# Transposing expert activations on VectorE in squares of 32, with ScalarE putting the squares together

## The chip, the cores and the metric

The kernel runs on one core of one Trainium2 chip. The metric is the time on the device in microseconds (us). Each number called "time before" is the median of three runs. Beside the runs there is one profiled execution, from which all durations of single instructions come.

## The reference, cut to what matters

The model is one block with two layers on an input of 4 x 1024 tokens of 1024 features. The first layer is a two-sided scan over time that gates a dense layer. The second layer, where the change lies, is a mixture of experts:

```python
logits = flat @ router_w.T                      # 4096 tokens, E = 32 experts
topk_w, topk_ids = lax.top_k(softmax(logits), 4)
xs = take(flat, tok_idx)                        # tokens sorted by expert
g, u = split(ragged_dot(xs, w1, group_sizes), 2)    # w1: 1024 x (2 * 512) per expert
act = silu(g) * u
ys = ragged_dot(act, w2, group_sizes)           # w2: 512 x 1024 per expert
routed = sum over a token's 4 experts of ys * topk_w
out = residual + routed + shared expert
```

Everything is in float32.

## The kernel before

The kernel has three stretches. In the first, up to about 1860 us, VectorE scans and TensorE computes the dense layer and the shared expert for most tokens. In the second, up to about 4644 us, the experts run. In the third, the shared expert of the last two chunks of tokens is computed.

The change is in the second stretch. Its work is cut into units. A **pair** unit (`kind` 0) takes two blocks of 128 tokens of one expert. A **single** unit (`kind` 1) takes one block. There are 68 pairs and 12 singles in a fixed list (`whole`): a single stands behind every fifth or sixth pair, and the last unit is a single. The instructions of each engine are written out by hand in the order in which that engine runs them (`manual_schedule`), so the order of the Python calls is the order on the queue of each engine.

A unit has these steps:

- `gather` fetches the tokens' rows from memory into `hs` (POOL's indirect DMAs, L904). `turn` transposes them on VectorE in squares of 32 into `hsT` (L1003). The rows are gathered in such an order that squares are enough there.
- `left_sums` forms sums of quarters of the transposed matrix (L1018 to L1022), four operations on VectorE: `s_up` from `hsT`, `s_down` from `actT`. Pairs need them because `products` multiplies two by two quarters with seven products instead of eight. `up_sums` (L870) and `down_sums` (L890) are the sums of the weights' quarters.
- `up` multiplies with w1 into the PSUM banks gA, gB and gC (L1151 for pairs, L1039 for singles), applies Silu on ScalarE (L1069, L1076, L1047), and multiplies the two halves and the token's share on VectorE (L1078, L1079, L1049). The result is `act`, 128 tokens x 512 features for each block.
- `turn_act` transposes `act`, so that the features lie on the partitions: four TensorE transposes of 128x128 for each block into a PSUM tile `tr` (L1088), and one copy on ScalarE to `actT` (L1089).
- `down` multiplies `actT` with w2 into the banks dA, dB and dC (L1151 for pairs, L1101 for singles). `add` scatters the result with an indirect DMA that adds (L1135).

In `products` (L1151) the seven products share three banks. A bank that holds a product is read by ScalarE as `m1` (L1165) or by VectorE as `u2` and `u3` (`u`, L1168 and L1174), and a later product is added into the same bank. So the second and the fourth product go to bank B, and the fourth waits until `u2` has been read out of it; the sixth takes bank A again.

`run_units` is the loop over units. It is a pipeline of two: while TensorE does `up` of unit u, VectorE works on the sums of the unit behind (`held`, whose `down` follows) and of the next one (`nxt`). The list `beside` says which steps of these sums are issued after each product of `up`. Before the change, for a pair, that is: after the first product two steps of `held.left` (the four `s_down`) and one of `held.down_sums`, after the second one more, after the third the last two, and after the fourth to the seventh one step of `nxt.up_sums` each. After `up` come the loads of w1 for the unit two ahead (SP's queue), `held.down()` with `nxt.turn()` beside it, the gather of the unit two ahead and `held.add()` on POOL, and then `turn_act` of unit u.

## Time and profile before

| What | us |
|---|---|
| Median of three runs | 4958.87 (4955.35 to 4960.45) |
| Profiled execution, its own time | 4949.14 |
| Its span | 4947.4 |
| TensorE busy (matmul) | 4654.2, 94% of the span |
| VectorE busy | 3395.2, 69% |
| ScalarE busy | 1268.3, 26% |
| Expert stretch 1850 to 4640: TensorE / VectorE / ScalarE / POOL busy | 2774.1 / 1914.7 / 304.1 / 848.4 |
| `tr` transposes of `act` on TensorE (L1088) | 592 instructions |
| `actT` copies on ScalarE (L1089) | 148 instructions, 589 ns each |

In the profile PE is TensorE, PEld its weight loads, DVE is VectorE, ACT is ScalarE, POOL is GpSimd and SP the engine that only issues DMAs. A row of a timeline gives the start, the time, the engine, the line and the operation with the tile written and the tiles read; in brackets stands how long the engine was idle before it and what ended that. A row of the chain of work that ended last gives start, time and instruction: it is followed back from the last instruction to what released it. A row of the waits gives who waited for whom: the total, the number of times and the longest.

### The profile page before, as it was taken

What the parts mean: (1) busy time and instruction counts of PE and PEld (TensorE: products, weight loads), DVE (VectorE), ACT (ScalarE), POOL (GpSimd) and SP (SyncE); (2) the same over time, 40 slices, a digit from 0 to 9 for tenths busy, and PEclk for the clock granted to TensorE, in tenths of its full rate; (3) what the DMA queues carried; (4) which work ended last, traced back from release to release, by engine and by line L of the source; (5) the groups of instructions that cost most, each with busy time, mean ns of one, the idle gap of its engine ahead of it and who ended that gap; (6) DMA issues with size and microseconds to landing.
All of it is one profiled execution on the core that took longest, in us unless ns stands there. A gap on an engine that the chain in (4) does not pass through costs nothing.

```text
span 4947.4 us, 34599 instructions
## 1 busy us (share of the span) xinstructions
PE 4654.2 (94%) x11638; PEld 2097.7 (42%) x11638; DVE 3395.2 (69%) x3579; ACT 1268.3 (26%) x1537; POOL 1230.7 (25%) x1209
## 2 busy tenths in 40 slices
PE   0379999999999999999999999999999999999999
PEld 0124444444444444444444444444444444444444
DVE  9988988898762227676767676676767676767434
ACT  5557656666451201111111111111111111111000
POOL 0013202401321212233332323233332323333000
PEclk9989999999999999999999999999999999999999
DMA  5688679669769565777777777777777777777623
GB/s 159 176 223 213 184 218 287 170 189 278 208 180 259 149 206 181 241 229 245 230 252 225 246 229 240 238 240 230 244 228 251 234 238 233 237 240 235 192 94 111
DMA packets 533886, 1071.37 MB, mean 217 GB/s; under 512 B 37537, under 2 KB 275234, under 8 KB 532866
## 3 DMA queue, kind: packets, MB, share of 16 engines
q1 hardware_dynamic: 364050, 736.31, 43.0%
q0 software_dynamic: 81760, 223.15, 21.8%
q10 hardware_dynamic: 87888, 109.59, 6.5%
q8 instruction: 94, 1.54, 0.1%
q14 instruction: 94, 0.77, 0.0%
HBM read 833.65 MB, written 205.65 MB: 210 GB/s over the span
## 4 chain that ended last, share of the span: by engine, by line
PE 85%; DVE 6%; DMA 3%; ACT 2%; issue 2%; SPq 0%; POOL 0%; ACTq 0%; DVEq 0%; POOLq 0%
PE gA L1151 15%; PE mm L660 11%; PE gC L1151 10%; PE gB L1151 10%; PE dA L1151 8%; PE mm L688 6%; PE dC L1151 6%; PE dB L1151 5%; PE mm L443 5%; PE gB L1039 2%; PE gA L1039 2%; PE tr L1088 1%; PE tr L544 1%; DVE fg L284 1%; DMA xg<-in_xT 1%
## 5 line engine op out<-in xcount | busy, mean ns | idle before, releaser
L904 POOL DMA_INDIRECT hs<-h_d,parts x584 | 591.3, 1012 | 1392.1 <-DVE hsT L1003 1237.9
L660 PE MATMUL mm<-c,wpc 128*128 128x512 f32 x1536 | 668.6, 594 | 0.0
L443 PE MATMUL mm<-c,w0t 128*128 128x512 f32 x1024 | 446.3, 597 | 209.0 <-DMA w0t<-in_w 205.8
L1151 PE MATMUL gC<-w,s_up 128*128 128x512 f32 x1184 | 532.3, 592 | 0.0
L1151 PE MATMUL gB<-t_up,s_up 128*128 128x512 f32 x1152 | 517.9, 592 | 0.0
L1151 PE MATMUL gA<-w,hsT 128*128 128x512 f32 x1088 | 491.3, 594 | 3.1 <-DVE hsT L1003 1.6
L660 PEld LDWEIGHTS mm<-c,wpc 128*128 128x128 f32 x1536 | 290.1, 191 | 356.1 <-issue 354.2
L1135 POOL DMA_INDIRECT sum_d<-y,tokens x148 | 269.3, 1820 | 589.7 <-DMA sum_d<-y,tokens 457.2
L443 PEld LDWEIGHTS mm<-c,w0t 128*128 128x128 f32 x1024 | 195.4, 192 | 456.2 <-issue 443.8
L688 PE MATMUL mm<-sact,wpc 128*128 128x512 f32 x768 | 342.5, 601 | 8.9 <-DMA wpc<-in_sd 5.7
L1151 PEld LDWEIGHTS gC<-w,s_up 128*128 128x128 f32 x1184 | 224.8, 190 | 282.2 <-issue 282.2
L1151 PEld LDWEIGHTS gB<-t_up,s_up 128*128 128x128 f32 x1152 | 218.9, 190 | 275.5 <-issue 261.6
L870 DVE TENSOR_TENSOR t_up<-w,w 128x2048 f32<-128x2048 f32 x136 | 310.6, 2284 | 0.0
L1151 PEld LDWEIGHTS gA<-w,hsT 128*128 128x128 f32 x1088 | 202.1, 191 | 232.5 <-issue 228.8
L296 DVE TENSOR_TENSOR_SCAN fg<-decay,tail,fg 128x1024 f32<-128x1024 f32 x128 | 292.7, 2328 | 0.0
L1151 PE MATMUL dB<-t_down,s_down 128*128 128x512 f32 x544 | 257.7, 596 | 9.7 <-DVE u L1168 9.7
L1151 PE MATMUL dA<-w,actT 128*128 128x512 f32 x544 | 255.6, 592 | 0.0
L1151 PE MATMUL dC<-w,s_down 128*128 128x512 f32 x544 | 255.6, 592 | 0.0
L329 POOL DMA_DIRECT2D fg<-euk x64 | 57.8, 904 | 772.9 <-DVE euk L328 509.2
L1151 PE MATMUL gA<-t_up,hsT 128*128 128x512 f32 x544 | 244.5, 592 | 0.0
L1076 ACT ACTIVATE act<-c 128x512 f32<-128x512 f32 x68 | 42.9, 630 | 708.9 <-DVE c L1072 708.9
L688 PEld LDWEIGHTS mm<-sact,wpc 128*128 128x128 f32 x768 | 145.1, 193 | 180.8 <-issue 172.8
(296 smaller groups left out, 6208.7 us busy)
## 6 DMA issues: line engine op xcount, KB each, us to landing
w<-in_w SPq DMA_DIRECT2D x240, 2048.0 KB, 8.5
fg<-euk POOLq DMA_DIRECT2D x64, 512.0 KB, 6.8
c_d<-r ACTq DMA_DIRECT2D x64, 512.0 KB, 7.7
w0t<-in_w SPq DMA_DIRECT2D x64, 512.0 KB, 6.5
c<-c_d SPq DMA_DIRECT2D x120, 256.0 KB, 6.6
wpc<-in_sg SPq DMA_DIRECT2D x48, 512.0 KB, 4.6
wpc<-in_su SPq DMA_DIRECT2D x48, 512.0 KB, 4.6
wpc<-in_sd SPq DMA_DIRECT2D x48, 512.0 KB, 6.2
```

The lines of the kernel that those rows point to most:

```text
L284: nc.vector.tensor_tensor_scan(fg[:, m, :], dk.to_broadcast([P, T]), x, 0.0, ALU.mult, ALU.add)
L296: nc.vector.tensor_tensor_scan(fg[:, m, ::-1], decay[L][:, ct, b : b + 1].to_broadcast([P, T]), fg[:, m, ::-1], tail[:, m : m + 1], ALU.mu ...
L329: nc.gpsimd.dma_start(out=num, in_=euk, accum_op=ALU.add)
L443: nc.tensor.matmul(mm, lhsT=tiles[ot][:, it, :], rhs=c0s[it], start=(it == 0), stop=(it == NC - 1))
L544: nc.tensor.matmul(lgT_ps, lhsT=rw_sb[:, ct, :], rhs=hs[ct], start=(ct == 0), stop=(ct == NC - 1))
L660: nc.tensor.matmul(mm, lhsT=wts[f, n][:, kt, :], rhs=c1s[q, kt], start=(kt == 0), stop=(kt == NC - 1))
L688: nc.tensor.matmul(mm, lhsT=wts[ct][:, f, :], rhs=acts[q, f], start=(f == 0), stop=(f == NSI - 1))
L870: nc.vector.tensor_tensor(to, x, y, ALU.subtract)
L904: nc.gpsimd.indirect_dma_start(out=to[:, bass.ts(g, C // SQ)], out_offset=None, in_=h_d.rearrange("t (q c) -> (t q) c", q=SQ), in_offset=b ...
L1039: nc.tensor.matmul(ps, lhsT=self.hsT[:, k, 0, :], rhs=w[k // NK][:, k % NK, bass.ts(n, I)], start=(k == 0), stop=(k == NC - 1),)
L1135: nc.gpsimd.indirect_dma_start(out=sum_d, out_offset=bass.IndirectOffsetOnAxis(ap=tokens[:, i, self.n : self.n + 1], axis=0), in_=y, in_of ...
L1151: nc.tensor.matmul(ps, lhsT=x[:, k, :], rhs=w[:, k, :], start=(k == 0 and not more), stop=(k == half - 1), skip_group_check=more,)
```

## The change

The activations are no longer transposed on TensorE. `turn_act` now issues one VectorE transpose for each block, of 128x512 in squares of 32, from `act` into the PSUM tile `tr`. A square stays within its 32 partitions, so ScalarE then copies from each of the four partition quadrants to each of four others: 16 copies of 32 partitions x 4 x 32 elements for each block, into `actT`. These copies are a generator, `together`, with eight steps for a pair and four for a single, each of four copies.

`run_units` issues the copies of `held` beside the `up` of the next unit: in a pair two steps after each of the first four products, in a single all steps after the two products. The `s_down` sums of `held`, which read `actT`, move from the first product to behind the sixth and the seventh, in both cases after that place's step of `up_sums`; in a single they move behind the second product. The `down_sums` move to behind the second and the third product.

```diff
             def turn_act(self):
                 self.actT = pxt.tile([P, NI, 2, P], FP, name="actT")
-                for b, act in enumerate(self.acts):
-                    tr = ps_t.tile([P, 4, P], FP, name="tr")
-                    for f in range(NI):
-                        nc.tensor.transpose(tr[:, f, :], act[:, bass.ts(f, P)], ident)
-                    nc.scalar.copy(self.actT[:, :, b, :], tr)
+                squares = []
+                for act in self.acts:
+                    squares.append(ps_t.tile([P, 4, P], FP, name="tr"))
+                    nc.vector.transpose(squares[-1].rearrange("p k t -> p (k t)"), act)
+
+                def together():
+                    for b, tr in enumerate(squares):
+                        of = tr.rearrange("p k (q j) -> p k q j", q=SQ)
+                        for r in range(SQ):
+                            for q in range(SQ):
+                                nc.scalar.copy(
+                                    self.actT[bass.ts(r, SIDE), :, b, bass.ts(q, SIDE)], of[bass.ts(q, SIDE), :, r, :]
+                                )
+                            yield
+
+                self.together = together()
                 self.left = self.left_sums(self.actT, ND, "s_down")
                 self.s_down = next(self.left, None)
...
-                jobs = [] if held is None else 2 * [held.left] + 4 * [held.down_sums]
+                jobs = [] if held is None else 4 * [held.down_sums]
+                left = [] if held is None else 2 * [held.left]
+                together = [] if held is None else 2 * [held.together]
                 sums = [] if nxt is None else 4 * [nxt.up_sums]
-                beside = [jobs + sums[:2], sums[2:]] if u.kind else [jobs[:3], jobs[3:4], jobs[4:]] + [[s] for s in sums]
+                if u.kind:
+                    beside = [2 * together + jobs + sums[:2], 2 * together + left + sums[2:]]
+                else:
+                    rest = [[s] for s in sums] if sums else [[] for _ in range(4)]
+                    beside = [together + x for x in ([], jobs[:2], jobs[2:], rest[0])] + [
+                        rest[1],
+                        rest[2] + left[:1],
+                        rest[3] + left[1:],
+                    ]
...
+            rest_of(held.together)
             rest_of(held.left)
             rest_of(held.down_sums)
```

## The prediction

> **What bounds the kernel now.** I read the page first: engine shares, then the chain of work that ended last.

> ```profile
> PE 4654.2 (94%) x11638; PEld 2097.7 (42%) x11638; DVE 3395.2 (69%) x3579; ACT 1268.3 (26%) x1537; POOL 1230.7 (25%) x1209
> PE 85%; DVE 6%; DMA 3%; ACT 2%; issue 2%; SPq 0%; POOL 0%; ACTq 0%; DVEq 0%; POOLq 0%
> ```

> TensorE bounds the kernel. The expert loop runs from 1859 to 4644 us, and between 1850 and 4640 TensorE is busy 2774.1 of 2790 us at clock 1.00, VectorE 1914.7, ScalarE 304.1. So every TensorE microsecond taken out counts, and so does every wait put in. The removed transposes, by their line, then the chain through the end of one pair unit and the start of the next (start, length):

> ```profile
> L1088 PE MATMUL tr<-ident,act x592: 272/273/421, 1885.4 to 4635.9; 128*128 128x128 f32 x198
> ```
> ```profile
> 2723.72 1.72 PE dA L1151 x4
> 2725.44 1.74 PE dB L1151 x4
> ...
> 2732.33 0.88 PE tr L1088 x8
> 2733.21 3.43 PE gA L1151 x8
> 2736.64 3.43 PE gB L1151 x8
> ```

> Eight transposes hold the chain for 0.88 us, not 8 x 0.273: they overlap, at 0.11 us each. All the rest of a pair unit is products back to back: seven of 3.43 (up), seven of 1.72 (down). Where would a wait bite? From the table of waits and the timeline of VectorE beside those products:

> ```profile
> PEld dB L1151 <- DVE u L1168: 44.5, 55, 1.7
> ```
> ```profile
> 2716.90 0.69 DVE L1072 TENSOR_TENSOR c<-u,gA 128x512 f32<-128x512 f32 x1 [0.54 <-PE gA L1151]
> 2717.50 2.28 DVE L870 TENSOR_TENSOR t_up<-w,w 128x2048 f32<-128x2048 f32 x1
> 2720.33 0.69 DVE L1072 TENSOR_TENSOR c<-u,gC 128x512 f32<-128x512 f32 x1 [0.55 <-PE gC L1151]
> 2720.93 0.75 DVE L1078 SCALAR_TENSOR_TENSOR act<-act,shares,c 128x512 f32<-128x512 f32 x1
> 2721.60 0.75 DVE L1079 SCALAR_TENSOR_TENSOR act<-act,shares,c 128x512 f32<-128x512 f32 x1
> 2722.26 2.29 DVE L870 TENSOR_TENSOR t_up<-w,t_up 128x2048 f32<-128x2048 f32 x1
> 2724.46 0.68 DVE L1168 TENSOR_TENSOR u<-m,dB 128x512 f32<-128x512 f32 x1
> ...
> 2732.37 0.69 DVE L1123 TENSOR_TENSOR y<-u,dC 128x512 f32<-128x512 f32 x1 [1.03 <-PE dC L1151]
> 2732.97 0.68 DVE L1018 TENSOR_TENSOR s_up<-hsT 128x512 f32<-128x512 f32 x1
> 2733.69 0.69 DVE L1019 TENSOR_TENSOR s_up<-s_up,hsT 128x512 f32<-128x512 f32 x1
> ...
> 2735.51 0.41 DVE L1018 TENSOR_TENSOR s_down<-actT 128x256 f32<-128x256 f32 x1
> 2735.96 0.43 DVE L1019 TENSOR_TENSOR s_down<-s_down,actT 128x256 f32<-128x256 f32 x1
> 2736.30 0.42 DVE L1021 TENSOR_TENSOR s_down<-actT 128x256 f32<-128x256 f32 x1
> ```

> The reader is to see two tight places. First, the fourth down product (the second into bank dB) waits until `u` has been read out of dB; `u` ends at 2725.14, the product starts at 2725.28, and its weight load already waited. 55 such waits are 44 pair units at 0.58 (25.5 us, hidden: the chain shows 1.74 for 1.72) and 11 single units at 1.7. So in 44 pairs VectorE is exactly in time. Second, from c to `u` VectorE runs without a gap: whatever is put there arrives late at TensorE. The start-to-start steps are 0.60 for an operation of 512 columns, 0.34 for one of 256 (0.45 if it needs the one before), 2.20 after one of 2048.

> **The change part by part.**

> *Transposes gone from TensorE: -63.1 us.* 67 pairs x 0.87 (from 2732.17, where TensorE starts the first of the eight, to gA at 2733.04) plus 11 singles x 0.44 = 58.3 + 4.8 = 63.1. The first pair gains nothing: its next product waits for hsT anyway (1.56 us, "PE gA <- DVE hsT"). The last single is priced below.

> *left_sums moved from the start of the next unit to its sixth and seventh product: +33 us.* In the changed program VectorE's order there is c, t_up, two s_down, c, act, act, t_up, two s_down, `u`. Counted from 2716.90: t_up +0.60 (2717.50), s_down +2.20 (2719.70), +0.45 (2720.15), next c 2720.49 instead of 2720.33; then 0.60, 0.67, 0.66, 2.20 to the third s_down (2724.62), 0.34, 0.34: `u` starts 2725.30 instead of 2724.46, ends 2725.98. The product starts 0.06 after `u` (as at 2095.29 and 2095.35 in a single), so 2726.04 instead of 2725.28: 0.76, call it 0.75. 44 x 0.75 = 33. Behind `u` on VectorE wait the two hsT transposes and the second `u`; they shift with the product (2728.19 against its end at 2727.9), so this is not paid twice. The 12 pairs ahead of a single have no up_sums (TensorE keeps VectorE waiting there), the 11 behind a single have no left_sums: no price.

> *VectorE's transposes, two per pair ahead of s_up: +2 us.* They stand behind y (2732.37), where TensorE's first gA now starts at 2732.17. The nearest row is hsT (L1003): 1221 ns for 1024 columns, as a TENSOR_TENSOR of that size, so 512 columns should take 0.69, step 0.60. Then s_up 2734.17, its second 2734.89, end 2735.58, gB at 2735.64 against 2735.60: 0.04 x 44 = 2. No row shows VectorE writing PSUM. Below: 0 (gB can't start before gA ends). Above: no overlap, step 0.69, 0.22 x 44 = 10. I take 0.04, since reading PSUM costs nothing (688 against 683 ns). Singles and pairs behind them have over 0.5 us of room.

> *ScalarE's copies, 16 per block, 2368 in all.* Nearest rows: 589 ns for 128x512 (L1089), 212 for 128x16 (L223), the same 575 on 32 partitions as on 128; by the line through them a 32x4x32 copy takes 0.30 us. Two in a row:

> ```profile
> 2732.81 1.07 ACT L1089 COPY actT<-tr 128x512 f32<-128x512 f32 x2 [6.74 <-PE tr L1088]
> ```

> Two of 0.59 in 1.07: they overlap by 0.11, so the step of small ones is 0.19 to 0.20. [...]

> [...]

> *Singles: +16 us.* Here all 32 copies and left_sums sit between the second up product and `u`:

> ```profile
> 2089.42 0.75 DVE L1049 SCALAR_TENSOR_TENSOR act<-act,shares,gB 128x512 f32<-128x512 f32 x1 [2.14 <-PE gB L1039]
> ...
> 2094.61 0.68 DVE L1168 TENSOR_TENSOR u<-m,dB 128x512 f32<-128x512 f32 x1
> ```

> The unit begins at 2075.41. ScalarE's Silu starts 7.07 in, copies from 7.6 to 7.6 + 32 x 0.20 = 14.0. VectorE is free at 14.68, so left_sums don't wait, and the copy m behind the copies is due only at 15.7. left_sums put 1.47 (0.45 + 3 x 0.34) ahead of the two t_up and `u`, on which dB already waits. 11 x 1.47 = 16. At a step of 0.29 the copies end at 16.9 and add 2.25 each, 25 more: 0.22 is the break point. [...]

> *The last single: +3.6 us.* Nothing runs on TensorE beside its 16 copies: y at 4635.74, transpose +0.60 to 4637.03, copies to 4640.4, dA there instead of 4636.85.

> *Nothing:* down_sums moved behind the first `u` (4 x 1.25 from 7.7 to 12.7, the second `u` is due at 13.9; were that 1.2 us of room gone, `u` and the c behind it would be late by the rest); the two PSUM tiles, which the copies free 16 us into a unit at the latest; the other queues: SP's w loads and POOL's gathers and adds keep their order and their waits on the same products, with hs gathered a unit ahead.

> Sum: -63.1 + 33 + 2 + 16 + 3.6 = -8.5 us. The profiled execution took 4949.1 (span 4947.4), 9.7 under the median 4958.87; I put the difference on the median: 4950.

> **The rivals.**
> 1. *The copies don't overlap (slower).* Place: singles, left_sums waiting for actT. Price: 352 x (step - 0.22) + 16 x (step - 0.20); at 0.29 +26, so 4976. It cancels the gain from 0.24 us a copy, and is visibly slower from 0.27. [...] Against: the overlap of the pair of copies.
> 2. *VectorE has more room than counted (faster).* If `u` were not late in the pairs, 33 us come back: 4917; with the singles too, 4901. For it: VectorE is 69% busy. Against: the 0.58 us waits at just this product.
> 3. *VectorE's transposes into PSUM are dear.* Each 0.1 us above 0.60 puts 0.2 on 44 pairs, 8.8 us in all: 4959, no change; at 0.9 a piece 26 us.
> The program's order excludes that the change does nothing: no TensorE transpose is left in the experts.

> **How the numbers follow.** About 0.2% (9.9 us) is what a measurement of this kernel can tell from no change. My forecast (step 0.20, transposes 0.60 to 0.69, stall 0.65 to 0.85) runs from -14 to +4 and has 0.58: 0.26 faster, 0.32 same. Rival 1: 0.20, of it 0.15 slower and 0.05 same. Rival 2: 0.09, faster. Rival 3 and other costs of small copies: 0.13, of it 0.10 slower. Sums: faster 0.35, same 0.40, slower 0.25. Range 4936 to 4978: it reaches into rival 2 a little and holds rival 1 at 0.29.

> **What would show it.** In the profile after: no `tr` of acts on PE; `PE dB <- DVE u` some 44 times near 0.75 us (33 us) and 11 near 2.5; the ACT group of 2368 copies with 16 of them in about 3.2 us; s_down in singles waiting on ACT not at all; gA right behind dC. A step of 0.29 shows as s_down waiting on ACT actT for 2.2 us in singles. The forecast is wrong if dB waits are absent in pairs, or gB waits for s_up by over 0.3.

## The result, and the profile after

The changed kernel takes 4978.59 us (median of five runs, 4977.05 to 4984.94). The kernel before, run on the same chip in the same rounds, takes 4955.35 (4953.64 to 4960.45). The ratio is 1.0051, with a 95% interval of 1.0040 to 1.0062: the change makes the kernel half a per cent slower. The forecast was 4950, with a range that ended at 4978.

The first lines of the page after, busy time and groups:

```profile
PE 4619.9 (93%) x11046; PEld 2034.8 (41%) x11046; DVE 3482.4 (70%) x3727; ACT 1781.8 (36%) x3757; POOL 1213.6 (24%) x1209
...
L1097 ACT COPY actT<-tr 32x128 f32<-32x128 f32 x2368 | 606.7, 256 | 33.9 <-DVE tr L1090 7.7
...
L1164 PE MATMUL dB<-t_down,s_down 128*128 128x512 f32 x544 | 269.3, 618 | 66.8 <-DVE u L1181 48.8
```

TensorE lost its 592 transposes and is busy for less time; ScalarE has 2368 small copies in place of 148 whole ones. The span is 4975.9 where it was 4947.4. (Lines moved: the products of `products` are now L1164, `u` L1181.) The chain view of this run reaches back over the last 6% of the span only, so the reading below goes by waits and timelines.

Waits in the expert stretch (who waits for whom: total, times, longest):

```profile
PEld dB L1164 <- DVE u L1181: 94.3, 55, 2.9
PE dB L1164 <- DVE u L1181: 48.8, 55, 2.1
PEld gB L1164 <- DVE s_up L1019: 33.8, 55, 0.7
PE dB L1164 <- DVE s_down L1019: 18.0, 12, 1.5
DVE s_down L1018 <- ACT actT L1097: 17.0, 12, 1.4
PE dA L1114 <- ACT actT L1097: 5.8, 1, 5.8
```

The first two lines are the wait that was forecast. The fourth and fifth are not: in twelve places, the single units, VectorE waits 1.4 us for ScalarE's copies, and TensorE waits behind it.

**A pair unit.** TensorE in the timeline (start, time, instruction, idle before; a row overlaps the next by 0.16, so a down product that isn't held is 1.72 from start to start):

```profile
2692.27 1.88 PE L1164 MATMUL dA<-w,actT 128*128 128x512 f32 x4
2694.73 1.98 PE L1164 MATMUL dB<-t_down,s_down 128*128 128x512 f32 x4 [0.59 <-DVE u L1181]
2696.55 1.88 PE L1164 MATMUL dC<-w,s_down 128*128 128x512 f32 x4
...
2701.70 3.60 PE L1164 MATMUL gA<-w,hsT 128*128 128x512 f32 x8
2705.18 3.70 PE L1164 MATMUL gB<-t_up,s_up 128*128 128x512 f32 x8
2708.72 3.60 PE L1164 MATMUL gA<-w,hsT 128*128 128x512 f32 x8
```

VectorE and ScalarE beside it:

```profile
2694.00 0.68 DVE L1181 TENSOR_TENSOR u<-m,dB 128x512 f32<-128x512 f32 x1
...
2702.51 1.31 DVE L1090 STREAM_TRANSPOSE tr<-act 128x512 f32<-128x512 f32 x2
2703.73 0.67 DVE L1018 TENSOR_TENSOR s_up<-hsT 128x512 f32<-128x512 f32 x1
2704.43 0.69 DVE L1019 TENSOR_TENSOR s_up<-s_up,hsT 128x512 f32<-128x512 f32 x1
```
```profile
2705.38 0.59 ACT L1178 COPY m<-gA 128x512 f32<-128x512 f32 x1 [10.61 <-PE gA L1164]
2705.86 4.28 ACT L1097 COPY actT<-tr 32x128 f32<-32x128 f32 x16
```

The second dB would have started at 2692.27 + 1.72 = 2693.99 and starts at 2694.73: `u`, which ends at 2694.68, makes it 0.74 late. (The bracket says 0.59 because the row before overlaps it.) The product then takes 1.98 instead of 1.88, and the next starts 1.82 behind it. gB has the same: 3.48 behind gA instead of 3.43, and then 3.70 long instead of 3.60. And the sixteen copies take 4.28 us, a step of (4.28 - 0.26) / 15 = 0.268 us.

**A single unit.** ScalarE, VectorE and TensorE of one (from 2075.24 to 2105.11):

```profile
2082.80 8.58 ACT L1097 COPY actT<-tr 32x128 f32<-32x128 f32 x32
```
```profile
2089.24 0.75 DVE L1049 SCALAR_TENSOR_TENSOR act<-act,shares,gB 128x512 f32<-128x512 f32 x1 [2.47 <-PE gB L1039]
2091.41 0.42 DVE L1018 TENSOR_TENSOR s_down<-actT 128x256 f32<-128x256 f32 x1 [1.42 <-ACT actT L1097]
...
2097.41 0.68 DVE L1181 TENSOR_TENSOR u<-m,dB 128x512 f32<-128x512 f32 x1
```
```profile
2092.35 1.98 PE L1164 MATMUL dB<-t_down,s_down 128*128 128x512 f32 x4 [1.50 <-DVE s_down L1019]
2098.14 1.98 PE L1164 MATMUL dB<-t_down,s_down 128*128 128x512 f32 x4 [2.10 <-DVE u L1181]
```

All 32 copies end at 2091.38. VectorE is free at 2089.99 and sits idle for 1.42 us. The first dB would have started at 2088.97 + 1.72 = 2090.69 and is 1.66 late for it; `u` and the second dB are late with it. The unit takes 29.87 us; before it took 27.34, and there the second dB waited 0.89 us:

```profile
2095.35 1.98 PE L1151 MATMUL dB<-t_down,s_down 128*128 128x512 f32 x4 [0.89 <-DVE u L1168]
```

In four of the eleven singles it is 31.57, and there the product behind the second wait looks like this (TensorE's timeline in another single, then both singles in the view of stretches: length, busy time and count of each engine, granted clock, DMA share, GB/s):

```profile
2343.18 3.65 PE L1164 MATMUL dB<-t_down,s_down 128*128 128x512 f32 x4 [2.09 <-DVE u L1181]
2346.67 1.88 PE L1164 MATMUL dC<-w,s_down 128*128 128x512 f32 x4
```
```profile
2098.00:2102.00 4.00, 3.86 (x9) 1.82 (x10) 3.06 (x5) 0.00 (x0) 2.01 (x2) 1.00 0.88 345
2343.00:2347.00 4.00, 3.82 (x5) 1.70 (x6) 2.54 (x4) 0.00 (x0) 2.02 (x2) 0.57 0.86 340
```

The same product after the same wait takes 3.65 us instead of 1.98, at a granted clock of 0.57 instead of 1.00. In the last single, where TensorE waits for 5.81 us, the same happens:

```profile
4662.57 6.20 PE L1114 MATMUL dA<-w,actT 128*128 128x512 f32 x8 [5.81 <-ACT actT L1097]
4668.61 3.60 PE L1114 MATMUL dB<-w,actT 128*128 128x512 f32 x8
```

The first pair of the stretch lost the clock too, behind a wait of 1.52 us that both kernels have (before, then after):

```profile
1859.01 3.70 PE L1151 MATMUL gA<-w,hsT 128*128 128x512 f32 x8 [1.52 <-ACT rT L694]
1860.00:1864.00 4.00, 4.00 (x11) 1.85 (x10) 1.50 (x3) 0.59 (x1) 0.00 (x0) 1.00 0.21 62
```
```profile
1857.79 5.40 PE L1164 MATMUL gA<-w,hsT 128*128 128x512 f32 x8 [1.52 <-ACT rT L694]
1860.00:1864.00 4.00, 4.00 (x9) 1.76 (x8) 0.28 (x1) 0.59 (x1) 0.00 (x0) 0.77 0.00 0
```

The same gA takes 1.70 us longer, at a granted clock of 0.77 instead of 1.00.

**The account.** A unit's length is taken from its first gA to the next unit's. Summed by kind over the expert stretch of the two profiled executions (the first pair aside), with what the prediction's steps give for the same units:

| Units | before | after | difference | predicted |
|---|---|---|---|---|
| 44 pairs between pairs | 1627.64 | 1630.23 | +2.6 | -3.3 |
| 12 pairs ahead of a single | 443.09 | 434.35 | -8.7 | -10.4 |
| 11 pairs behind a single | 349.52 | 339.90 | -9.6 | -9.6 |
| 11 singles | 300.76 | 335.36 | +34.6 | +11.2 |
| the last single | 34.04 | 42.95 | +8.9 | +3.6 |
| sum | | | +27.7 | -8.5 |

Against the prediction's steps the units miss by 36.2 us, and two thirds of it (23.4) are in the eleven singles. The spans of these two executions differ by 28.5: the 27.7 of the table, 1.7 in the first pair, and -0.9 around the experts, which begin 1.2 earlier. The medians differ by 23.2.

### The profile page after: what moved, and what is told of

It is laid out like the page before. It is cut to its first block, busy times and chain, and to the rows that moved or that the text cites. A ratio compares the mean times of both kernels' runs of the same rounds, so it can differ in the third digit from the quotient of the medians.

```text
span 4975.9 us, 35734 instructions
## 1 busy us (share of the span) xinstructions
PE 4619.9 (93%) x11046; PEld 2034.8 (41%) x11046; DVE 3482.4 (70%) x3727; ACT 1781.8 (36%) x3757; POOL 1213.6 (24%) x1209
## 5 line engine op out<-in xcount | busy, mean ns | idle before, releaser
L1097 ACT COPY actT<-tr 32x128 f32<-32x128 f32 x2368 | 606.7, 256 | 33.9 <-DVE tr L1090 7.7
L1164 PE MATMUL gC<-w,s_up 128*128 128x512 f32 x1184 | 532.2, 592 | 0.0
L1164 PE MATMUL gB<-t_up,s_up 128*128 128x512 f32 x1152 | 522.4, 596 | 0.0
L1164 PE MATMUL gA<-w,hsT 128*128 128x512 f32 x1088 | 492.6, 596 | 7.0 <-DVE hsT L1003 5.5
L1148 POOL DMA_INDIRECT sum_d<-y,tokens x148 | 250.5, 1692 | 607.4 <-DMA sum_d<-y,tokens 474.6
L1164 PEld LDWEIGHTS gC<-w,s_up 128*128 128x128 f32 x1184 | 224.8, 190 | 282.2 <-issue 282.2
L1164 PEld LDWEIGHTS gB<-t_up,s_up 128*128 128x128 f32 x1152 | 215.2, 190 | 285.7 <-issue 249.2
L1164 PE MATMUL dB<-t_down,s_down 128*128 128x512 f32 x544 | 269.3, 618 | 66.8 <-DVE u L1181 48.8
L1178 ACT COPY m<-gA 128x512 f32<-128x512 f32 x74 | 43.4, 586 | 778.6 <-PE gA L1164 778.6
L1164 PEld LDWEIGHTS gA<-w,hsT 128*128 128x128 f32 x1088 | 207.8, 191 | 269.4 <-issue 261.4
L870 DVE TENSOR_TENSOR t_up<-w,w 128x2048 f32<-128x2048 f32 x136 | 310.6, 2284 | 0.0
L1164 PE MATMUL dC<-w,s_down 128*128 128x512 f32 x544 | 255.6, 592 | 0.0
L1164 PE MATMUL dA<-w,actT 128*128 128x512 f32 x544 | 255.6, 592 | 0.0
L1164 PE MATMUL gA<-t_up,hsT 128*128 128x512 f32 x544 | 244.5, 592 | 0.0
```

The costliest lines, as they stand in the source:

```text
L870: nc.vector.tensor_tensor(to, x, y, ALU.subtract)
L1097: nc.scalar.copy(self.actT[bass.ts(r, SIDE), :, b, bass.ts(q, SIDE)], of[bass.ts(q, SIDE), :, r, :])
L1148: nc.gpsimd.indirect_dma_start(out=sum_d, out_offset=bass.IndirectOffsetOnAxis(ap=tokens[:, i, self.n : self.n + 1], axis=0), in_=y, in_of ...
L1164: nc.tensor.matmul(ps, lhsT=x[:, k, :], rhs=w[:, k, :], start=(k == 0 and not more), stop=(k == half - 1), skip_group_check=more,)
L1178: nc.scalar.copy(m1, pa_)
```

## The experiments

Each kernel is compared with the kernel before in the same rounds on the same chip; its time stood at 4951.6 to 4955.35 in them. Diffs are against the changed kernel. "Typical pair" is the most frequent length of a pair between pairs in the profiled execution, "single" the length of the singles that ran at the full clock, and "clock lost" how many of the eleven singles had a product at a lower granted clock behind the second wait (1.7 us more each).

| Kernel | us | ratio (95%) | typical pair | single | clock lost |
|---|---|---|---|---|---|
| before | 4955.35 | 1 | 36.95 | 27.34 | 0 |
| after | 4978.59 | 1.0051 (1.0040 to 1.0062) | 37.05 | 29.87 | 4 |
| 1 single: copies early | 4967.73 | 1.0027 (1.0016 to 1.0037) | 37.05 | 28.37 | 7 |
| 2 s_up first | 4980.34 | 1.0054 (1.0041 to 1.0068) | 36.90 | 29.85 | 7 |
| 3 pair: s_down early | 4942.27 | 0.9974 (0.9965 to 0.9982) | 36.22 | 29.88 | 3 |
| 4 the order alone | 5016.44 | 1.0126 (1.0111 to 1.0142) | 37.8 | 28.81 | 4 |
| 5 single: s_down first | 4939.83 | 0.9975 (0.9965 to 0.9985) | 37.05 | 26.90 | 0 |
| 6 all places | 4895.48 | 0.9888 (0.9873 to 0.9903) | 36.07 | 26.90 | 0 |
| 7 and the last on TensorE | 4888.61 | 0.9872 (0.9857 to 0.9887) | 36.07 | 26.90 | 0 |
| 8 two blocks in one copy | 4977.11 | 1.0049 (1.0033 to 1.0064) | 37.2 | 28.37 | 9 |
| 9 banks in turn | 4956.14 | one run | 37.05 | 28.37 | 0 |
| 10 quadrants in turn | 4977.77 | one run | 37.05 | 29.85 | 4 |
| 11 all partitions | 4961.67 | one run | 37.05 | 28.37 | 8 |
| 12 one source quadrant | 4977.36 | one run | 37.05 | 29.90 | 3 |

### Where the copies stand in a single (1)

```diff
                 if u.kind:
-                    beside = [2 * together + jobs + sums[:2], 2 * together + left + sums[2:]]
+                    step(*(4 * together))
+                    beside = [jobs + sums[:2], left + sums[2:]]
```

The copies are issued ahead of the single's `up`, so they begin while gA is still being computed.

> Changed kernel, but in a single unit all 32 copies stand ahead of the Silu on ScalarE (from about 2 us into the unit), the s_down sums stay where they are. Theory A (the loss is lateness: copies at a step of 0.268 us end 1.5 us after VectorE is free, so u and the second dB are late, and the long idle of TensorE drops its clock): s_down waits for no copy, the second dB starts about 1.5 us earlier in 11 singles (16 us), no product of a single at a lower clock (7 us), the first dB of the last single 1.5 us earlier: 4979 - 25 = 4954. Theory B (the copies cost by their number, as traffic beside TensorE and VectorE, wherever they stand): 4979.

Measured: 4967.73. VectorE's `s_down` in this kernel no longer waits for the copies, and the single is 1.50 shorter: 16.5 us. But the second wait is still 2.10 us, and now seven singles lose the clock instead of four (+5.1). -16.5 + 5.1 = -11.4, and the medians differ by -10.9 (the last single, 1.8 shorter, comes on top, and the start of the experts varies). VectorE's and TensorE's timelines in the same single as above:

```profile
2094.53 0.42 DVE L1018 TENSOR_TENSOR s_down<-actT 128x256 f32<-128x256 f32 x1
```
```profile
2101.26 2.92 PE L1164 MATMUL dB<-t_down,s_down 128*128 128x512 f32 x4 [2.10 <-DVE u L1181]
2103.97 2.69 PE L1164 MATMUL dC<-w,s_down 128*128 128x512 f32 x4
```

The first row has no bracket: the wait for ScalarE was real and is gone. The other two show that the loss of the clock does not hang on that wait: here the loss is spread over two products (2.92 and 2.69 instead of 1.98 and 1.88, which is 1.75). That no single would lose the clock once this wait was gone was the part of the expectation that failed.

### s_up ahead of the transposes (2)

```diff
-                u.turn_act()
                 if nxt is not None:
                     rest_of(nxt.left)
+                u.turn_act()
```

> Changed kernel, but VectorE's two transposes of act stand behind the four s_up sums instead of ahead of them. Theory A: the first gB no longer waits (0.05 and 0.10 to get going again, 56 pairs): 4979 - 8 = 4971; the copies still start in time, since ScalarE's m is due later than the transposes. Rival: TensorE's slower gA to gB has another cause (reads of the same tiles, PSUM writes by VectorE), and nothing moves: 4979.

Measured: 4980.34, no gain. Inside the units the edit did what it should: no gB waits for `s_up`, and the typical pair went from 37.05 to 36.90, 0.05 for the lateness of gB and 0.10 for the product behind the wait, which is 3.60 again. Over the 44 pairs and the 12 ahead of singles that is 6.3 us in a table of units like the one above. It was lost elsewhere: seven singles instead of four lost the clock (+4.9 in the sum of the singles), and in this execution the experts began at 1862.76 instead of 1857.79 (+5.0), of which 1.7 came back in the first pair, which kept the clock here; the last single was 0.8 shorter. The sum is +1.1, the difference of the two spans (4977.1 and 4975.9). The start of the experts lies between 1856.6 and 1864.0 in the profiled executions of this study, in code that no edit touches. So the mechanism is shown by the units, and the time by itself shows nothing.

### s_down early in the pairs (3), and the new order with the old transposes (4)

```diff
-                    beside = [together + x for x in ([], jobs[:2], jobs[2:], rest[0])] + [
-                        rest[1],
-                        rest[2] + left[:1],
-                        rest[3] + left[1:],
-                    ]
+                    beside = [4 * together + jobs[:2], jobs[2:] + left] + [[]] + rest
```

> Changed kernel, but in pairs all 32 copies stand directly behind m (the Silu behind them), two down_sums go back to the first product, and the s_down sums stand behind the other two, ahead of the second u; singles as changed. Theory A: the second dB no longer waits in 44 pairs, 0.74 and 0.10 each: 4979 - 37 = 4942. Rival (the wait only moves: the Silu is 2.5 us later, the second u 0.3 us): gC, gA or the c sums are late by the same, 4975 to 4985.

Measured: 4942.27. The typical pair takes 36.22, which is 0.83 less: about 0.74 for the late `u` and 0.10 for the product behind it. The waits of this kernel:

```profile
DVE s_down L1018 <- ACT actT L1097: 153.1, 68, 2.6
PE dB L1164 <- DVE u L1181: 23.1, 11, 2.1
```

VectorE now waits 153 us for the copies. 136 of it lie in 56 pairs, 2.4 us in each, and there it costs nothing: this wait ends while the unit has room. The other 17 are the twelve singles, which this kernel leaves as they were, 1.42 us each, and there it costs time. Of the 55 waits at dB 11 are left.

Experiment 4 has the new `beside`, but `turn_act` as before the change: four TensorE transposes and one whole copy for each block.

```diff
-                squares = []
-                for act in self.acts:
-                    squares.append(ps_t.tile([P, 4, P], FP, name="tr"))
-                    nc.vector.transpose(squares[-1].rearrange("p k t -> p (k t)"), act)
...
+                for b, act in enumerate(self.acts):
+                    tr = ps_t.tile([P, 4, P], FP, name="tr")
+                    for f in range(NI):
+                        nc.tensor.transpose(tr[:, f, :], act[:, bass.ts(f, P)], ident)
+                    nc.scalar.copy(self.actT[:, :, b, :], tr)
+                self.together = iter(())
```

> Kernel before with TensorE's transposes and whole copies, but down_sums and s_down sums in the places of the changed kernel. Theory A: the second dB waits in 44 pairs as in the changed kernel (0.84 each, 37 us) and u is 1.5 us later in 11 singles (16 us), gB does not wait: 4955 + 53 = 5008. Theory B (the small copies make the loss, the places are harmless): 4955 to 4960.

Measured: 5016.44. The waits of this kernel at dB are those of the changed one, with no small copy in it:

```profile
PE dB L1154 <- DVE u L1171: 48.9, 55, 2.1
```

The 44 pairs take 36.3 us more than before the change, 0.83 each; the singles take 22.9 more, 1.47 each and four times the clock. So the new places of the sums alone cost some 60 us, and taking the transposes from TensorE in the same order gains 37.9 against this kernel, not 63.1. In the sums of units the changed kernel loses 16.5 us against the 63.1 to the copies in the singles, 8.7 in the last single, and 6.7 to the waits for `s_up` behind VectorE's transposes; part of it doesn't show in the time, since in the profiled execution of experiment 4 the experts began 5.8 us later.

### The sums first in a single too (5), all places together (6), the last single on TensorE (7)

```diff
                 if u.kind:
-                    beside = [2 * together + jobs + sums[:2], 2 * together + left + sums[2:]]
+                    step(*(4 * together))
+                    beside = [jobs + sums[:2] + left, sums[2:]]
```

> Changed kernel, but in a single all 32 copies stand ahead of the Silu and the four s_down sums ahead of the multiplication of act, in a gap of VectorE; pairs as changed. Theory A (u late by the sums and copies put ahead of it; a wait of 2.1 us at the second dB is long enough to lose the clock): the wait of the second dB falls back to the 0.9 us of the kernel before, no product of these 11 singles runs at a lower clock, a single takes 26.9 us instead of 29.9 or 31.6: 4979 - 39 - 2 = 4938. Theory B (the clock falls with the amount of work on ScalarE, not with TensorE's idle time): products at the lower clock remain, 4950 or more.

Measured: 4939.83. The single is 26.90, 0.44 less than before the change: exactly the four transposes that left TensorE. No single loses the clock. The waits at dB in this kernel:

```profile
PE dB L1164 <- DVE u L1181: 35.6, 55, 0.9
```

The longest wait is 0.9 instead of 2.1.

Experiment 6 joins 2, 3 and 5.

> All three moves together (s_up ahead of the transposes, s_down early in pairs, copies and s_down early in singles). Theory A: the gains add up, 8 + 37 + 41: 4979 - 86 = 4893, faster than the kernel before by 62, nearly what the removed transposes took (63). Rival: with all waits gone something else is late by the same (POOL's gathers, loads of w), 4920 or more.

Measured: 4895.48. A pair takes 36.07, 0.88 less than before the change. What is left is the last single, 40.58 us instead of 34.04, where TensorE has nothing to do while ScalarE puts the squares together. Experiment 7 leaves that one block on TensorE:

```diff
-            def turn_act(self):
+            def turn_act(self, whole=False):
...
+                if whole:
+                    tr = ps_t.tile([P, 4, P], FP, name="tr")
+                    for f in range(NI):
+                        nc.tensor.transpose(tr[:, f, :], self.acts[0][:, bass.ts(f, P)], ident)
+                    nc.scalar.copy(self.actT[:, :, 0, :], tr)
...
-                u.turn_act()
+                u.turn_act(nxt is None and u.kind == 1)
```

> As the one before, but the very last single is transposed by TensorE with one copy, as before the change. Theory A: the 6 us of idle TensorE ahead of its dA go, and with them the lower clock of that product (2.5 us): 7 us less, 4886. Rival: nothing of it shows in the end, 4893.

Measured: 4888.61 (4887.02 to 4892.39), against 4951.81 before in the same rounds. The last single is 34.04 again. The page and the waits:

```profile
PE 4589.3 (94%) x11050; PEld 2036.3 (42%) x11050; DVE 3481.5 (71%) x3726; ACT 1784.1 (37%) x3742; POOL 1233.6 (25%) x1209
```
```profile
DVE s_down L1018 <- ACT actT L1102: 144.6, 57, 3.2
PE dB L1169 <- DVE u L1186: 9.7, 11, 0.9
```

This version beats both kernels, by 63.2 us or 1.28% (1.13 to 1.43) against the one before. The prediction put the removed transposes at 63.1: all of it can be had. The units alone, without the start of the experts, which varies, give 63.6. ScalarE's copies are as slow as in the changed kernel, and VectorE waits 144.6 us for them, but in no place where TensorE then waits.

### Why the copies don't overlap (8 to 12)

In the changed kernel a copy runs 0.257 us and the next starts 0.268 after it: no overlap, where two copies of 128x512 overlapped by 0.11. What separates them? Size, bank and partition quadrant were the candidates. Experiment 8 puts both blocks of a pair into one tile of two banks, and one copy moves 256 columns for both:

```diff
...
+                            nc.scalar.copy(
+                                self.actT[bass.ts(r, SIDE), :, 0:nb, bass.ts(q, SIDE)],
+                                of[bass.ts(q, SIDE), :, 0:nb, r, :],
+                            )
...
```

> Changed kernel, but one copy takes a square of both blocks (32 partitions x 256 columns), 16 copies a pair instead of 32. What it tells: the step from copy to copy, 0.268 us at 128 columns and 0.48 at 512. Theory floor (an instruction cannot follow in under 0.27): step 0.27 at 256. Theory no overlap (step is the duration, 0.257 at 128): 0.37. Either way the copies of a single end before VectorE is free, so s_down waits for none and 1.5 us go in 11 singles; the 2.1 us wait at the second dB stays, with or without a lower clock behind it: 4955 to 4970.

ScalarE's timeline in a pair of it:

```profile
2707.63 5.98 ACT L1096 COPY actT<-tr 32x256 f32<-32x256 f32 x16
```

A copy twice as wide takes 0.362 us and has a step of (5.98 - 0.362) / 15 = 0.374: its own length again, without overlap. The 32 copies of a pair (8.58 us) became 16 in 5.98, and the single lost 1.50 as in experiment 1. The time did not follow: 4977.11, since nine singles lost the clock and a pair took 0.17 more: from VectorE's first transpose to its first `s_up` it is 1.39 us here and 1.22 in the changed kernel, and gB starts 3.64 behind gA instead of 3.48.

Experiment 9 takes the copies of the two blocks in turn, so that the bank changes with every copy and the quadrants with every second one. Experiment 10 changes both quadrants with every copy.

```diff
-                    for b, tr in enumerate(squares):
-                        of = tr.rearrange("p k (q j) -> p k q j", q=SQ)
-                        for r in range(SQ):
-                            for q in range(SQ):
+                    ofs = [tr.rearrange("p k (q j) -> p k q j", q=SQ) for tr in squares]
+                    for r in range(SQ):
+                        for q in range(SQ):
+                            for b, of in enumerate(ofs):
...
```

> Changed kernel, but in pairs one copy reads the PSUM bank of the first block and the next that of the second, in turn. What it tells: why small copies don't overlap (step 0.268 at a length of 0.257) while whole ones do (0.48 at 0.59), those two having read two banks. Theory bank (two copies in a row from one bank can't overlap): the step falls to about 0.16 to 0.20, and the 32 copies of a single take about 6 us instead of 8.6. Theory size (a short copy leaves nothing to overlap): step 0.27 as it is.

```diff
-                        for r in range(SQ):
+                        for d in range(SQ):
                             for q in range(SQ):
+                                r = (q + d) % SQ
```

> Changed kernel, but copies in a row write to different partition quadrants (as they already read from different ones). Theory quadrant (two copies in a row into one quadrant can't overlap): step 0.16 to 0.20. Theory size: 0.27.

ScalarE's timelines of experiment 9 and of experiment 10:

```profile
2703.06 3.42 ACT L1098 COPY actT<-tr 32x128 f32<-32x128 f32 x16
```
```profile
2705.96 4.27 ACT L1098 COPY actT<-tr 32x128 f32<-32x128 f32 x16
```

In 9 the steps alternate: 0.16 between two copies with the same quadrants and another bank, 0.27 where a quadrant changes. In 10 all are 0.27, as after. So a change of bank is not what holds a copy back. In 9 TensorE waits in a single for the copies ahead of dA, 0.39 us, and then 1.70 for `u`, where it waited 2.10 in one piece in experiment 1. The singles are as long as there, 28.37, and none loses the clock:

```profile
2099.99 1.99 PE L1167 MATMUL dB<-t_down,s_down 128*128 128x512 f32 x4 [1.70 <-DVE u L1184]
```

Experiment 11 copies all 128 partitions at once, from start partition 0 to start partition 0. The squares stay in their partitions, so it does not compute the layer, and only its time is read:

```diff
-                                nc.scalar.copy(
-                                    self.actT[bass.ts(r, SIDE), :, b, bass.ts(q, SIDE)], of[bass.ts(q, SIDE), :, r, :]
-                                )
+                                nc.scalar.copy(self.actT[:, :, b, bass.ts(q, SIDE)], of[:, :, r, :])
```

> Changed kernel, but each of the 16 copies moves 128 partitions x 4 x 32 without a change of quadrant, so the squares land in wrong places: only its time is of use. Theory partitions (copies of 32 partitions, or across quadrants, are what doesn't overlap): step 0.16 to 0.20. Theory size: 0.27.

And experiment 12 swaps the two loops, so that the source's quadrant stays for four copies and the destination's changes each time (after the change it is the other way round):

```diff
-                        for r in range(SQ):
-                            for q in range(SQ):
+                        for q in range(SQ):
+                            for r in range(SQ):
```

> Changed kernel, but four copies in a row read from one partition quadrant and write to the four others (the changed kernel reads from four and writes to one). What it tells: which quadrant, when it changes, keeps a copy from starting before the one ahead has ended. Theory source: the step is 0.16 three times and 0.27 the fourth, 0.19 on average, 32 copies in 6.0 us. Theory destination or either: 0.27 each time, 32 copies in 8.6 us, as with both changing.

ScalarE's timelines of experiment 11 (a pair's block) and of experiment 12 (a single's two blocks):

```profile
2700.50 2.82 ACT L1097 COPY actT<-tr 128x128 f32<-128x128 f32 x16
```
```profile
2084.84 8.60 ACT L1097 COPY actT<-tr 32x128 f32<-32x128 f32 x32
```

Copies of four times as many elements take two thirds of the time: in 11 the last of the sixteen starts at 2702.86, a step of (2702.86 - 2700.50) / 15 = 0.16, and no start partition changes there. So smallness does not keep copies from overlapping. Holding the source's quadrant alone buys nothing: 0.27. So in these runs a copy started only behind the end of the one before (a step of 0.27 at a length of 0.26) when either the source or the destination started in another quadrant; it was enough that one of them did (the source in the changed kernel, the destination in experiment 12). Where neither did, the step was 0.16.

## Why the prediction was wrong

What held, in the prediction's own steps:

- *Transposes gone, -63.1.* Right. In experiment 6 a pair is 0.88 shorter and in experiment 5 a single 0.44; experiment 7 gained 63.2 in all.
- *`u` late by 0.75 in 44 pairs.* Measured 0.74, in just those pairs; experiment 3 took it away.
- *VectorE's transposes, 0.69 with a step of 0.60, gB 0.04 late.* Measured 0.684 and 0.61 on average, gB 0.05 late. Rival 3 falls.
- *Nothing in the sum for the copies in pairs.* Right: TensorE's waits in pairs are for `u` and `s_up`, and in experiment 3 even 136 us in which VectorE waited for copies in pairs were free.
- *left_sums ahead of `u` in singles, 1.47 each.* Right: 28.37 with all 32 copies out of the way (experiments 1, 8 and 11) against 26.90 with the sums first (experiment 5).

What failed is the step "ScalarE's copies". I took 0.20 by the overlap of two copies of 128x512, and held the upper end, 0.29, for the less likely. No run shows the 0.29 that the upper end of the range and rival 1's 4976 go by; the runs showed 0.268 in its place. Between copies that change quadrant there was no overlap (a step of 0.268 at a length of 0.257), and no row of the trace before had two such copies in a row. The step is 0.268, above the break point of 0.22: the copies of a single end 16.1 us into the unit and not at 14.0, VectorE is free at 14.7, and `s_down` waits. The duration of 0.30 was too long as well (0.257): its line went through a copy of 128x512 out of PSUM (589 ns) and an activation of 128x16 in SBUF, the memory of all tiles outside PSUM (L223, 212 ns).

Rival 1 had the fact, the place and the price: at 0.268 its own formula gives 352 x 0.048 + 16 x 0.068 = 18.0. Its reason, that small copies don't overlap, is not the one: in experiments 9 and 11 they do (a step of 0.16). That its 4976 lies near the measured 4978.59 is in part luck. With the step as measured it gives 4968, and the rest came from terms that it did not have. The account of the miss, +27.7 against -8.5:

| us | where from |
|---|---|
| 16.4 | 11 singles, each 1.49 longer because `s_down` waits for copies (gone in experiment 1) |
| 6.8 | 4 singles x 1.70: the clock is lowered behind a wait of 2.1 (0.57 in the stretch) |
| 5.3 | the last single: 1.66 at its first dB, since it too has the 32 copies of the pair ahead of it, which the prediction had not counted; 16 x 0.068 for its own copies; 2.5 for the lower clock |
| 7.6 | the pairs, as measured: 44 x 0.10 for the product behind the wait for `u`, and 0.15, lateness and product, for the wait for `s_up` in 33 of them and in the 12 ahead of a single (4.4 + 6.7, less the 2 predicted for it); the other steps came out 1.5 better than predicted |
| 36.1 | of 36.2 |

The second row and the fourth were in no rival. The prediction priced a wait at its length. A wait of TensorE for VectorE cost 0.10 more each time (1.98 for 1.88, 3.70 for 3.60), and where it lasted 2.1 us another 1.7 in 49 of 99 cases. In these runs an idle time of 2.1 us was enough in three to nine of eleven singles, and the 1.52 us ahead of the first pair in two of fourteen executions; 1.70 us was not in any of eleven singles (experiment 9), nor 0.9 us in any.

What decided it for a given unit can be read from the same traces. In nine kernels (the changed one and 1, 2, 3, 4, 8, 10, 11 and 12) the eleven singles have the wait of 2.1 us: 99 waits, 49 with a loss. Take a period, divide the start of the product behind each wait by it and keep the remainder. Of all periods from 1 to 12 us, in steps of 0.0005, one alone, 3.4135, parts all nine executions: the units that lost the clock lie together in one stretch of the period, and those that kept it in the other. The changed kernel has 1.35, 1.39, 1.43 and 1.52 lost, and seven from 2.09 to 2.95 kept; experiment 10 has 1.28, 1.34, 1.39 and 1.48 lost, and 1.53, 1.60, 2.12, 2.22, 2.27, 2.36 and 2.87 kept. So in these runs the loss hung on where the wait fell in a period of about 3.41 us. The eleven waits of 1.70 us in experiment 9 are spread over the whole period, and none lost the clock.

So the change is slower because of where it puts things, not because of what it does: the sums `s_down` behind the sixth product in pairs and behind the copies in singles. With them elsewhere, `s_up` ahead of VectorE's transposes and the last single left on TensorE, it is 63.2 us faster (experiment 7).

## What to carry to other kernels

An overlap read from two large instructions (0.11 us here) did not carry over to many small ones that address other partitions (0.27 from start to start at a length of 0.26): look for a pair in the trace with the same change of start partition, or take no overlap. When work is moved to idle engines, place it by due times: on the engine that feeds the bottleneck put first what the bottleneck waits for next, and let the waits for the slow helper fall where there is room (144.6 us of such waits cost nothing in the best version). And when a wait on TensorE is priced, add what comes behind it: here 0.10 us for each, and for a wait of 2.1 us the 1.7 us of a lower clock in every second case (49 of 99).
